# A fused cross-attention kernel: the loop's steps in a new order, the values of block 29 in other PSUM banks, and a new order on the way out

## The chip, the core and the metric

The kernel runs on one core of one Trainium2 chip. The metric is device time in microseconds (us) of one execution, the median of three. The core's engines are called PE (TensorE, matrix products), DVE (VectorE), ACT (ScalarE), POOL (GpSimd) and SP (SyncE, whose queue issues nearly all DMAs here). Each engine works off its own instructions in the order in which they were written; instructions of different engines are tied by semaphores alone.

## What is computed

Sixteen sequences of 1024 rows and 512 features (`x`) attend to a context of 64 rows each. Queries come from `x`, keys and values from the context, both after a layer norm whose scale and shift are made from a conditioning vector. There are 16 heads of 32 features. The result is projected and added to `x`. All is float32.

```python
xq  = ada_ln(x_q,  silu(t) @ Wss_q  + bss_q)
xkv = ada_ln(x_kv, silu(t) @ Wss_kv + bss_kv)
q   = (xq @ Wq + bq).reshape(B, Lq, 16, 32)
k,v = split(xkv @ Wkv + bkv)
scores = einsum('bqhd,bkhd->bhqk', q, k) / sqrt(32)
out = einsum('bhqk,bkhd->bqhd', softmax(scores), v).reshape(B, Lq, 512)
return x_q + (out @ Wp + bp)
```

## The kernel before, in words

The queries are cut into 32 blocks of 512 rows (two for each sequence), called by their numbers 0 to 31. A block goes through these stages:

- **load and norm**: `load_x` (1 MB by DMA), `q_stats` (DVE), `q_scale` (ACT, then four tiny POOL operations), `hidden` (ACT, four pieces).
- **turn**: `turn` (DVE, four pieces) transposes 32x32 squares into the tile `ht`, of which there is one. `move` (16 DMAs of 64 KB on SP's queue) carries `ht` into the tile `xt` of turned features, of which there are two. `scale_features` (ACT, four pieces) applies scale and shift to `xt`, and `feature_sums` (POOL, four pieces) forms the sums and differences for the next stage.
- **queries**: the 512x512x512 product is made of seven half-size products (Strassen-Winograd). `query_product(n, k)` for k = 1 to 7 is one of them on PE, called q1 to q7 here. They are summed in two PSUM banks: q1, q6, q5 and q3 in bank 0; q2, and after it q7 and q4, in bank 1. `query_seed` (ACT) copies bank 0 into bank 1 between q1 and q2. `query_out` (ACT) and `query_added` (DVE) take the results to the tiles `qt`. q7 begins a new sum in bank 1, so it has to wait for `query_out(n, 2)`, which reads q2's result there.
- **scores**: `score_products` (PE) for halves w = 0 and 1 into the PSUM pool `ps_s` (two tiles of two banks each). `copied` and `copied_bank` bring them to SBUF (ACT, one quarter on DVE), `maximum` and `maximum_copied` (DVE) take maxima, `exchanged` (ACT) and `maxima` (DVE, with a spread to full size) finish them, `subtract` (POOL) subtracts, `weights` (ACT) is the exponential, `row_total` (DVE) the sums, `sums_moved` (five DMAs), `inverse` and `spread_rows` (DVE) the reciprocals.
- **values**: `mix` (PE) multiplies weights and values. In the loop its four results go to the four product banks (`apart=False`), before the loop and after it to the two tiles of `ps_s`. `divided_bank` or `divided` (DVE) multiplies with the reciprocals into the tile `ot`.
- **projection**: again seven half-size products, `product(b, k)`, p1 to p7 here, with `row_sums` (POOL) for their operands, `biased` and `product_seed` (ACT) to fill banks ahead, and `take` (ACT) with `joined` (POOL), or `added` (DVE), to add results to the residual tile `r`. `joined` of 4 and `added` of 3 also issue the stores.

After a start of 142 us in which the stages fill, a loop of 28 steps works on five blocks at a time. In step `i` it has a = i-1 (second half of the scores, softmax), b = i-2 (values, projection), n = i+1 (queries), f = i+2 (features scaled and summed) and i+3 (norm, turn, move). The order of the calls is written out by hand and kept as written. What follows the loop, for blocks 29 to 31, is called the tail; there y = 30 and z = 31.

On PE a step is: scores of a (second half), mix of b, scores of i (first half), then seven q and seven p in some order, with q3 at the end. `move` of a step cannot begin before q3, which still reads the tile that it fills; SP's queue holds it back until then, and all that SP has behind it.

Of the kernel before, what the change touches and what calls it, by code (L numbers as in the profile page):

```python
# [20 lines left out]
def cross_attention_block(  # L21
# [729 lines left out]

    def weights(i, w):
        p = s_tiles[i, w]
        nc.scalar.activation(p, p, AF.Exp, scale=SCALE)  # L754
# [686 lines left out]
    for i in range(3, NB - 1):  # L1441
# [53 lines left out]
        if next_x:
            q_stats(i + 4, (3,))
        if more:
            turn(i + 3, (1,))
        maximum(i, 0, 1)
        weights(a, 1)  # L1500
        joined(b, 2, 0)
        row_total(a, 1)
        product(b, 6)
        product(b, 7)
        if i == NB - 3:
            load_residual(NB - 1)
        take(b, 6, 2)
# [5 lines left out]
        query_added(n, 5)
        sums_moved(a)
        if more:
            turn(i + 3, (3,))
        take(b, 7, 1)
        joined(b, 6, 2)
        exchanged(i, 0)
        if more:  # L1520
            turn(i + 3, (0,))
        if more:
            turn(i + 3, (2,))
        joined(b, 7, 1)
        take(b, 5, 3)
        if f < NB:
            scale_features(f, (2,))
        if f < NB:
            scale_features(f, (3,))
        joined(b, 5, 3)  # L1530
        if f < NB:
            feature_sums(f, nc.gpsimd, (0,))
        if next_x:
            q_stats(i + 4, (0,))
# [31 lines left out]
    maximum(y, 1, 0)
    copied(y, 1, 0)
    maximum(y, 1, 1)
    exchanged(y, 1)
    weights(y, 0)  # L1570
    biased(y - 1, 2)
    mix(y - 1)
    maxima(y, 1)
    divided(y - 1, (1,))
    divided(y - 1, (0,))
    row_total(y, 0)
# [145 lines left out]
```

## Time and profile before

| what | number |
|---|---|
| time, median of three runs | 1009.05 us (1008.04 to 1010.91) |
| time of the profiled execution | 1009.7 us |
| its span, first to last instruction | 1007.9 us |
| mean granted clock of PE | 0.995 |
| PEld busy (weight loads, beside PE) | 767.2 us (76%) |
| DVE busy | 927.2 us (92%) |
| ACT busy | 781.3 us (78%) |
| POOL busy | 852.8 us (85%) |
| start, to the first step of the loop | 0 to 142.35 us |
| loop, 28 steps | 142.35 to 944.53 us |
| tail | 944.53 us to the end |

Busy shares are means over stages. Whether an engine bounds a stage is read from stretches of the time line: from the length of one step, from what an engine waited for, and from what released it. The profile names instructions by line, output and input; buffer numbers are left out in it (`pq` is any bank of a query product, `pp` of a projection product, `ps` scores, `po` values, `mb` the spread maxima, `lt` the row sums).

### The profile page before, as it was taken

The numbers are of one execution on the slowest core, as the hardware profiler recorded it, in microseconds if no ns is written. First come the engines' busy times: TensorE is split into PE (matmuls) and PEld (weight loads), VectorE is DVE, ScalarE is ACT, GpSimd is POOL, SyncE is SP. The second block draws the span as 40 slices with busy tenths as digits, with TensorE's granted clock in tenths as the row PEclk, the third lists the DMA queues.
The fourth block names the chain that finished last, engine by engine and source line by source line (L and its number), as shares of the span: only waits on it lengthen the run. The fifth ranks groups of instructions, "written<-read, shape, count | busy, mean of one in ns | idle before, by whom it ended". The sixth has DMA issues, their size and how long they took to land.

```text
span 1007.9 us, 18000 instructions
## 1 busy us (share of the span) xinstructions
PE 987.9 (98%) x6088; PEld 767.2 (76%) x6088; DVE 927.2 (92%) x1221; ACT 781.3 (78%) x1459; POOL 852.8 (85%) x635
## 2 busy tenths in 40 slices
PE   8999999999999999999999999999999999999888
PEld 6878777787777777877777778777777788777567
DVE  6789999999999999999999999999999999887885
ACT  3689768788788888888888788888888888866550
POOL 2566688899999998999998899999999999988684
PEclk9999999999999999999999999999999999999899
DMA  9584553444544544545444545455444544443113
GB/s 322 181 228 132 160 182 108 155 155 147 161 139 143 153 159 158 165 137 167 149 144 133 161 160 164 135 166 154 148 132 161 160 158 128 131 128 129 47 48 131
DMA packets 111803, 151.71 MB, mean 151 GB/s; under 512 B 29624, under 2 KB 45008, under 8 KB 111712
## 3 DMA queue, kind: packets, MB, share of 16 engines
q1 hardware_dynamic: 111024, 149.75, 47.5%
q8 instruction: 48, 0.79, 0.3%
q0 software_dynamic: 256, 0.52, 0.2%
q14 instruction: 43, 0.35, 0.1%
q10 hardware_dynamic: 432, 0.30, 0.1%
HBM read 80.26 MB, written 35.65 MB: 115 GB/s over the span
## 4 chain that ended last, share of the span: by engine, by line
PE 63%; SPq 11%; DVE 8%; ACT 5%; POOL 5%; DMA 4%; issue 3%; DVEq 0%; POOLq 0%; ACTq 0%
PE pp L939 25%; PE pq L555 25%; SPq L402 10%; PE ps L675 4%; PE po L841 3%; DMA xt<-ht 2%; DVE lt L763 2%; POOL r L985 1%; ACT qt L596 1%; POOL xt L511 1%; POOL xt_sums L511 1%; PE pv_B L555 1%; PE pk_A L555 1%; ACT taken L980 1%; PE pk_B L555 1%
## 5 line engine op out<-in xcount | busy, mean ns | idle before, releaser
L750 POOL TENSOR_TENSOR s<-s,mb 128x2048 f32<-128x2048 f32 x64 | 290.8, 4543 | 26.2 <-DVE mb L733 23.8
L985 POOL TENSOR_TENSOR r<-r,taken 128x512 f32<-128x512 f32 x148 | 188.4, 1274 | 48.0 <-ACT taken L980 47.7
L939 PE MATMUL pp<-w_p_sb,ot 128*128 128x256 f32 x760 | 182.0, 384 | 0.0
L939 PEld LDWEIGHTS pp<-w_p_sb,ot 128*128 128x128 f32 x760 | 146.1, 193 | 22.9 <-issue 2.3
L763 DVE TRANSPOSE_TENSOR_REDUCE lt<-s 128x64 f32<-128x2048 f32 x64 | 146.3, 2286 | 8.8 <-ACT s L754 8.4
L733 DVE STREAM_TRANSPOSE mb<-m 128x2048 f32<-128x2048 f32 x64 | 147.9, 2311 | 6.7
L980 ACT COPY taken<-pp 128x512 f32<-128x512 f32 x148 | 86.7, 586 | 83.8 <-PE pp L939 83.0
L754 ACT ACTIVATE s<-s 128x2048 f32<-128x2048 f32 x64 | 122.2, 1910 | 11.7 <-POOL s L750 11.0
L555 PE MATMUL pq<-xt_sums,w_q_sums 128*128 128x256 f32 x512 | 122.3, 382 | 4.5 <-ACT qt L596 4.3
L555 PE MATMUL pq<-xt,w_q_sb 128*128 128x256 f32 x512 | 124.1, 385 | 0.0
L939 PE MATMUL pp<-WT,ot 128*128 128x256 f32 x512 | 121.2, 380 | 1.5 <-ACT pp L887 0.8
L555 PEld LDWEIGHTS pq<-xt,w_q_sb 128*128 128x128 f32 x512 | 94.7, 190 | 36.0 <-DVE ot L813 22.7
L939 PE MATMUL pp<-WT,s 128*128 128x256 f32 x512 | 121.0, 379 | 1.1 <-DVE r L964 1.1
L555 PE MATMUL pq<-xt,w_q_sums 128*128 128x256 f32 x512 | 121.0, 379 | 0.0
L596 ACT ACTIVATE qt<-pq,bias_t 128x256 f32<-128x256 f32 x256 | 106.5, 468 | 13.9 <-PE pq L555 13.9
L713 ACT COPY s<-ps 128x1024 f32<-128x1024 f32 x100 | 100.7, 1008 | 20.7 <-PE ps L675 17.4
L555 PEld LDWEIGHTS pq<-xt_sums,w_q_sums 128*128 128x128 f32 x512 | 96.0, 190 | 22.9 <-ACT qt L596 10.5
L460 ACT ACTIVATE xt<-xt,ss_q 128x512 f32<-128x512 f32 x124 | 97.8, 812 | 15.7 <-DMA xt<-ht 14.7
L939 PEld LDWEIGHTS pp<-WT,ot 128*128 128x128 f32 x512 | 97.0, 190 | 16.1 <-ACT pp L887 1.6
L939 PEld LDWEIGHTS pp<-WT,s 128*128 128x128 f32 x512 | 97.2, 190 | 15.2 <-issue 2.0
L555 PEld LDWEIGHTS pq<-xt,w_q_sums 128*128 128x128 f32 x512 | 97.3, 190 | 13.2
L351 ACT ACTIVATE x<-x,rstdq 128x512 f32<-128x512 f32 x128 | 97.6, 812 | 1.1 <-POOL rstdq L326 1.1
(175 smaller groups left out, 1694.6 us busy)
## 6 DMA issues: line engine op xcount, KB each, us to landing
x<-in_x_dram SPq DMA_DIRECT2D x32, 1024.0 KB, 5.2
r<-in_x_dram SPq DMA_DIRECT2D x32, 1024.0 KB, 5.1
out_dram<-r SPq DMA_DIRECT2D x62, 512.0 KB, 3.7
xt<-ht SPq DMA_DIRECT2D x488, 64.0 KB, 2.0
wss_kv<-in_L_xcond_Wss_kv_dram SPq DMA_DIRECT2D x4, 512.0 KB, 5.0
wss_q<-in_L_xcond_Wss_q_dram SPq DMA_DIRECT2D x4, 512.0 KB, 9.4
ltd<-lt SPq DMA_DIRECT2D x32, 64.0 KB, 1.5
vr<-ltd SPq DMA_DIRECT2D x126, 16.0 KB, 1.7
```

The costliest lines, as they stand in the source:

```text
L351: nc.scalar.activation(dst, src, AF.Identity, bias=rstd[:, 1, j : j + 1], scale=rstd[:, 0, j : j + 1])
L402: (nc.gpsimd if two and g % 2 else nc.sync).dma_start(xt[32 * k : 32 * k + 32, g], ht[32 * g : 32 * g + 32, k].rearrange("p c t b -> p c ( ...
L460: nc.scalar.activation(xt[:, :, c, :], xt[:, :, c, :], AF.Identity, scale=ss["q"][:, c, b : b + 1], bias=ss["q"][:, NC + c, b : b + 1],)
L555: nc.tensor.matmul(out_, lhsT=lhsT, rhs=rhs, start=new and m == 0 and c == 0, stop=c == HC - 1, skip_group_check=True,)
L596: nc.scalar.activation(dst, src, AF.Identity, bias=bq_t[:, o : o + 1])
L713: nc.scalar.copy(s_tiles[i, z][:, 2 * e : 2 * e + 2, :], s_banks[i, z][e])
L733: nc.vector.transpose(t, src.unsqueeze(2).to_broadcast([P, HPC * NJ, 32]))
L750: eng.tensor_tensor(s_tiles[i, w], s_tiles[i, w], mb_tiles[i, w], ALU.subtract)
L754: nc.scalar.activation(p, p, AF.Exp, scale=SCALE)
L763: nc.vector.tensor_reduce(lt_tiles[i][:, :, w, :], s_tiles[i, w].rearrange("p r (j a) -> p r j a", a=32), AX.X, ALU.add, apply_transpose=True,
L939: nc.tensor.matmul(acc[products_of(i, n)][:, t * HO : (t + 1) * HO], lhsT=rows[:, c, t * P : (t + 1) * P], rhs=cols[:, c, :], start=new an ...
L985: nc.gpsimd.tensor_add(r, r, taken[i][:, slot, :].rearrange("p (t h) -> p t h", t=2))
```

## The change

The change does not touch the start. It writes the calls of the loop and of the tail in another order, and changes three things beside it: block 29's values go to the product banks (`mix(y - 1, False)` with four calls of `divided_bank`), `divided_bank` gets the homes of the `ot` tiles that `divided` had, and there is a helper `subtracted` that nothing calls. The numbers and kinds of the loop's calls stay the same.

```diff
+    def subtracted(i, w, e):
+        rs = slice(2 * e, 2 * e + 2)
+        nc.vector.tensor_tensor(s_tiles[i, w][:, rs, :], s_banks[i, w][e], mb_tiles[i, w][:, rs, :], ALU.subtract)
...
     def divided_bank(i, w, d):
         if i not in ot_tiles:
-            ot_tiles[i] = opool.tile([P, NC, TB], F32, tag="ot", name=f"ot_{i}")
+            pool, tag = {NB - 3: (kvpool, "KA"), NB - 2: (big, "big2")}.get(i, (opool, "ot"))
+            ot_tiles[i] = pool.tile([P, NC, TB], F32, tag=tag, name=f"ot_{i}")
...
-        load_residual(a)
+        copied_bank(a, 1, 2, nc.scalar)
         copied(a, 1, 0)
         copied_bank(a, 1, 3, nc.vector)
-        copied_bank(a, 1, 2, nc.scalar)
         mix(b, False)
...
-    mix(y - 1)
+    mix(y - 1, False)
+    score_products(z, 0)
+    divided_bank(y - 1, 1, 1)
+    divided_bank(y - 1, 0, 0)
+    divided_bank(y - 1, 1, 0)
     maxima(y, 1)
-    divided(y - 1, (1,))
-    divided(y - 1, (0,))
```

**Place 1: PE in the step i = 22.** These are the first seven of the fourteen products of the step before the change; `pq_23_1` and `pq_23_2` are the banks of block 23's queries, `pp_20` those of block 20's projection, and the row with `pq_23_7` is q7.

```order
L555 MATMUL pq_23_1_6368<-xt_23_6028,w_q_sb_99 128x256 x4
L939 MATMUL pp_20_1_6376<-w_p_sb_102,ot_20_6352 128x256 x4
L555 MATMUL pq_23_1_6368<-xt_sums_544,w_q_sums_125 128x256 x4
L939 MATMUL pp_20_2_6399<-w_p_sb_102,ot_20_6352 128x256 x4
L555 MATMUL pq_23_2_6378<-xt_23_6028,w_q_sb_99 128x256 x4
L555 MATMUL pq_23_1_6368<-xt_23_6028,w_q_sums_125 128x256 x4
L555 MATMUL pq_23_7_6439<-xt_sums_544,w_q_sums_125 128x256 x4
```

The same seven places after the change (what was line 555 stays, the projection's line is now 944):

```order
L555 MATMUL pq_23_1_6364<-xt_23_6043,w_q_sb_99 128x256 x4
L944 MATMUL pp_20_1_6373<-w_p_sb_102,ot_20_6362 128x256 x4
L555 MATMUL pq_23_1_6364<-xt_sums_544,w_q_sums_125 128x256 x4
L555 MATMUL pq_23_2_6379<-xt_23_6043,w_q_sb_99 128x256 x4
L944 MATMUL pp_20_2_6396<-w_p_sb_102,ot_20_6362 128x256 x4
L944 MATMUL pp_20_1_6373<-WT_1309,s2_20_6430 128x256 x4
L555 MATMUL pq_23_7_6451<-xt_sums_544,w_q_sums_125 128x256 x4
```

q7 stays in seventh place; q2 moved from the fifth to the fourth, so that two products instead of one lie between q2 and q7, and q5 gave its place to p6. The other seven are p6, p7, p5, q4, p3, p4, q3 before, and p5, q5, p7, p3, q4, p4, q3 after.

**Place 2: ACT in the same step.** From `query_seed` to the exponential of the step's second half, before the change; L460 is `scale_features` of block 24, and the row of `qt_23_0` is `query_out(n, 2)`, for which q7 waits.

```order
L567 COPY pq_23_2_6378<-pq_23_1_6368 128x512
L742 COPY m2_21_1_6325<-m2_21_1_6325 32x64 x4
L893 COPY pp_20_2_6399<-pp_20_1_6376 128x512
L754 ACTIVATE s_21_0_6110<-s_21_0_6110 128x2048
L596 ACTIVATE qt_23_1_6412<-pq_23_1_6368,bias_t_119 128x2x4x32 x2
L980 COPY taken_20_6419<-pp_20_2_6399 128x512
L460 ACTIVATE xt_24_6283<-xt_24_6283,ss_q_473 128x4x128
L887 COPY pp_20_7_6431<-b_p_sb_101 128x512
L596 ACTIVATE qt_23_0_6411<-pq_23_2_6378,bias_t_119 128x2x4x32 x2
```

After the change the same stretch of ACT, on to the first `scale_features`:

```order
L596 ACTIVATE qt_23_1_6416<-pq_23_1_6364,bias_t_119 128x2x4x32 x2
L596 ACTIVATE qt_23_0_6415<-pq_23_2_6379,bias_t_119 128x2x4x32 x2
L985 COPY taken_20_6428<-pp_20_2_6396 128x512
L892 COPY pp_20_7_6432<-b_p_sb_101 128x512
L351 ACTIVATE x_25_6024<-x_25_6024,rstdq_6241 128x512
L985 COPY taken_20_6428<-pp_20_1_6373 128x512
L758 ACTIVATE s_21_1_6326<-s_21_1_6326 128x2048
L460 ACTIVATE xt_24_6298<-xt_24_6298,ss_q_473 128x4x128 x2
```

`scale_features` stood ahead of `query_out(n, 2)` and now stands six rows behind it. On SP the stores of `added(b, 3)` and `joined(b, 4)` and `load_x` now stand ahead of `move`, where before only `load_x` did.

**Place 3: DVE at the head of the tail.** Before the change, from the maxima of block 30 to the second row sums of block 30 (L824 is `divided`, both banks of a half at once):

```order
L691 TENSOR_REDUCE m2_30_1_8482<-ps_30_1_0_8472 128x32
L691 TENSOR_REDUCE m2_30_1_8482<-ps_30_1_1_8473 128x32
L724 TENSOR_REDUCE m_30_1_8513<-m2_30_1_8482 128x64
L733 STREAM_TRANSPOSE mb_30_1_8515<-m_30_1_8513 128x2048
L824 TENSOR_TENSOR ot_29_8517<-po_29_1_8496,vb_29_8468 128x1024
L824 TENSOR_TENSOR ot_29_8517<-po_29_0_8495,vb_29_8468 128x1024
L763 TENSOR_REDUCE lt_30_8520<-s_30_0_8327 128x4x16
L691 TENSOR_REDUCE m2_31_0_8533<-ps_31_0_0_8523 128x32
L691 TENSOR_REDUCE m2_31_0_8533<-ps_31_0_1_8524 128x32
L763 TENSOR_REDUCE lt_30_8520<-s_30_1_8483 128x4x16
```

After the change (L818 is `divided_bank`, one bank at a time):

```order
L691 TENSOR_REDUCE m2_30_1_8484<-ps_30_1_0_8474 128x32
L691 TENSOR_REDUCE m2_30_1_8484<-ps_30_1_1_8475 128x32
L818 TENSOR_TENSOR ot_29_8526<-po_29_1_1_8497,vb_29_8468 128x512
L818 TENSOR_TENSOR ot_29_8526<-po_29_0_0_8494,vb_29_8468 128x512
L818 TENSOR_TENSOR ot_29_8526<-po_29_1_0_8496,vb_29_8468 128x512
L724 TENSOR_REDUCE m_30_1_8530<-m2_30_1_8484 128x64
L733 STREAM_TRANSPOSE mb_30_1_8532<-m_30_1_8530 128x2048
L691 TENSOR_REDUCE m2_31_0_8524<-ps_31_0_1_8515 128x32
L691 TENSOR_REDUCE m2_31_0_8524<-ps_31_0_0_8514 128x32
L818 TENSOR_TENSOR ot_29_8526<-po_29_0_1_8495,vb_29_8468 128x512
L767 TENSOR_REDUCE lt_30_8552<-s_30_0_8323 128x4x16
```

The divisions moved ahead of the spread maxima of block 30, but the one of `po_29_0_1` moved behind the maxima of block 31; p1 of block 29 reads it in its second matmul. On PE the order of the tail's head is the same in both: scores of 30, mix of 29, scores of 31, p1.

More of the change, by code (lines that the diff above doesn't have):

```diff
@@ L1497, in cross_attention_block @@
         if more:
[L1498 to L1507, printed above, removed]
+            turn(i + 3, (0,))
+        take(b, 5, 3)
         query_out(n, 7)
+        query_added(n, 5)
+        take(b, 7, 1)
+        product(b, 3)
         row_sums(b, 1, (1,))
-        product(b, 5)
+        joined(b, 6, 2)
+        joined(b, 7, 1)
+        if more:
+            turn(i + 3, (3,))
+        maxima(i, 0)
+        if next_x:
+            q_scale(i + 4)
+        sums_moved(a)
+        if f < NB:
+            scale_features(f, (1,))
+        query_product(n, 4)
+        product(b, 4)
         if f < NB:
             scale_features(f, (0,))
[L1513 to L1521, printed above, removed]
+        joined(b, 5, 3)
+        copied(i, 0, 1)
+        copied(i, 0, 0)
+        if f < NB:
+            feature_sums(f, nc.gpsimd, (0,))
+        query_added(n, 4)
         if more:
             turn(i + 3, (2,))
[L1524 to L1534, printed above, removed]
+        added(b, 3)
         if f < NB:
@@ L1582, in cross_attention_block @@
+    maxima(y, 1)
+    biased(y - 1, 2)
     copied(z, 0, 1)
     maximum(z, 0, 1)
-    weights(y, 1)
-    take(y - 1, 1, 0)
-    row_total(y, 1)
-    exchanged(z, 0)
-    row_sums(y - 1, 0, (1,))
-    copied(z, 0, 0)
-    row_sums(y - 1, 1, (0,))
-    maxima(z, 0)
-    joined(y - 1, 1, 0)
+    maximum(z, 0, 0)
+    subtract(y, 1)
+    divided_bank(y - 1, 0, 1)
+    row_sums(y - 1, 0, (0,))
+    row_sums(y - 1, 0, (1,))
+    weights(y, 0)
+    exchanged(z, 0)
+    weights(y, 1)
+    row_sums(y - 1, 1, (0,))
@@ L1602, in cross_attention_block @@
-    biased(y, 2)
     maximum(z, 1, 0)
-    biased(y - 1, 3)
-    product(y - 1, 7)
-    copied(z, 1, 0)
-    maximum(z, 1, 1)
-    exchanged(z, 1)
-    inverse(y)
-    row_sums(y - 1, 1, (1,))
-    product(y - 1, 5)
-    take(y - 1, 5, 1)
+    exchanged(z, 1)
+    maxima(z, 1)
+    inverse(y)
+    joined(y - 1, 2, 1)
+    row_sums(y - 1, 1, (1,))
+    copied(z, 1, 0)
+    copied(z, 1, 1)
+    subtract(z, 1)
+    take(y - 1, 5, 1)
+    mix(y)
+    spread_rows(y, (0,))
+    weights(z, 0)
+    take(y - 1, 7, 2)
@@ L1613, in cross_attention_block @@
+    spread_rows(y, (1,))
+    divided(y, (0,))
+    divided(y, (1,))
     product(y - 1, 3)
[L1614 to L1617 removed]
     product(y - 1, 4)
[L1619 to L1633 removed]
@@ L1634, in cross_attention_block @@
[L1634 to L1655 removed]
+    row_total(z, 0)
+    weights(z, 1)
+    row_total(z, 1)
@@ new lines, in cross_attention_block @@
+    product(y, 1)
+    product(y, 2)
+    added(y, 1)
+    added(y, 2)
+    row_sums(y, 0, (0,))
+    biased(y, 3)
+    row_sums(y, 0, (1,))
+    mix(z)
+    joined(y - 1, 7, 2)
+    row_sums(y, 1, (0,))
+    row_sums(y, 1, (1,))
+    product(y, 6)
+    sums_moved(z)
+    product(y, 7)
+    added(y, 6)
+    added(y, 7)
+    joined(y - 1, 5, 1)
+    take(y - 1, 3, 2)
+    inverse(z)
+    product(y, 5)
+    biased(z, 2)
+    spread_rows(z, (0,))
+    take(y, 5, 1)
+    take(y - 1, 4, 0)
+    joined(y - 1, 6, 3)
@@ L1669, in cross_attention_block @@
-    product(z, 6)
     biased(z, 3)
-    row_sums(z, 1, (1,))
-    added(y, 3)
     product(z, 7)
@@ L1675, in cross_attention_block @@
     added(z, 7)
+    added(y, 3)
     product(z, 5)
+    product(z, 4)
     added(z, 5)
-    product(z, 4)
     product(z, 3)
```

170 lines of the change are left out of this document (74 added, 96 removed).

## The prediction

> All times are of the profiled execution: 1009.7 us, span 1007.9. It stood 0.65 us above the median of three (1009.05).
>
> **What bounds the kernel now.** I read the page's engine shares, then the stretches of the time line, then PE's own rows, then the waits, then the chain.
>
> ```profile
> PE 987.9 (98%) x6088; PEld 767.2 (76%) x6088; DVE 927.2 (92%) x1221; ACT 781.3 (78%) x1459; POOL 852.8 (85%) x635
> ```
> PE is busy 98% of the span, so there is little to gain: 20 us of idle in all. The stretches (length, then busy time of PE, PEld, DVE, ACT and POOL, then PE's granted clock) say where.
>
> ```profile
> 142.35:170.69 28.34, 28.34 (x177) 22.15 (x177) 27.44 (x38) 22.96 (x42) 23.75 (x20) 1.00 0.43 137
> 170.69:200.23 29.54, 28.60 (x177) 22.07 (x176) 28.03 (x36) 23.78 (x44) 26.13 (x20) 1.00 0.46 148
> 142.35:915.81 773.46, 768.98 (x4754) 596.76 (x4753) 737.90 (x928) 637.67 (x1172) 701.75 (x506) 1.00 0.48 149
> 915.81:944.53 28.72, 28.72 (x178) 22.33 (x177) 23.86 (x24) 17.57 (x31) 22.82 (x14) 1.00 0.23 78
> 944.53:982.47 37.94, 31.32 (x217) 17.81 (x217) 32.73 (x27) 22.56 (x34) 31.97 (x16) 0.87 0.18 59
> 945.68:982.33 36.65, 30.20 (x200) 17.55 (x200) 32.09 (x25) 21.73 (x32) 30.68 (x15) 0.86 0.18 61
> 982.47:1003.73 21.26, 21.25 (x96) 17.96 (x96) 12.90 (x17) 2.28 (x4) 11.27 (x10) 1.00 0.37 132
> ```
> The first two are the loop's first and second step, from one score product of PE to the next. The first takes 28.34 us with PE never idle: that is what PE's work of a step needs, the floor. The third row holds 27 steps: 773.46 - 27 x 28.34 = 8.28 us above the floor. The fourth is the last step: 28.72, 0.38 above. So the loop has **8.66 us** to give, no more.
>
> ```profile
> 142.35 1.11 PE L675 MATMUL ps<-qt,K_A 32*64 32x512 f32 x16
> 146.32 1.99 PE L555 MATMUL pq<-xt,w_q_sb 128*128 128x256 f32 x8
> 858.35 1.11 PE L675 MATMUL ps<-qt,K_B 32*64 32x512 f32 x16
> 886.68 1.11 PE L675 MATMUL ps<-qt,K_B 32*64 32x512 f32 x16
> 186.22 1.99 PE L555 MATMUL pq<-xt_sums,w_q_sums 128*128 128x256 f32 x8 [0.94 <-ACT qt L596]
> PE pq L555 <- ACT qt L596: 4.3, 9, 0.9
> ```
> The first two rows are the start of the loop and the first of its products, 3.97 later. From 858.35 to 886.68 is the last of eleven steps (of 27) at the floor, the first being that from 142.35. The row at 186.22 is q7, the seventh product of the second step. It waited 0.94 us for `query_out(n, 2)`. The last row, from the list of waits, is the only wait of PE in the loop: 9 times 4.3 us together; the rest of the 8.28 us is the refill after it and waits too short to be listed. The chain shows what holds it, in the step from 743.59:
>
> ```profile
> 743.96 0.28 SPq L402
> ...
> 754.10 2.06 DMA xt<-ht
> ...
> 756.38 0.81 ACT xt L460
> 757.20 0.48 ACT pp L887
> 757.68 0.77 ACT qt L596 x2
> ...
> 758.49 1.56 PE pq L555 x6
> ```
> `move` begins when q3 of the step before is done, issues sixteen DMAs in 10.1 us, and the last lands 2.06 us later. `scale_features` waits for it on ACT, and the `query_out` that q7 needs stands behind it in ACT's queue.
>
> **The change in the loop.** Set a step's start at 0. PE's fourteen products fill the time from 3.97 to 28.34, 1.74 each (1.73 from start to start), and q7 is seventh in both orders, at 14.5. Before, `query_out(n, 2)` stood behind a landing at 12.2 to 13.4; now it stands behind the first exponential, q2 and nothing of the move. On ACT: the seed copy after q1 (6.0 to 6.6), `exchanged` to 7.65, two pieces to 8.95, `weights(a, 0)` to 10.9, two `query_out` to 12.5: 2 us before q7. `scale_features` now follows `weights(a, 1)`, at 17.3 at the earliest. So this stall goes: **-8.28, and -0.38** for the last step, whose move is long over. What is late next decides whether the floor is reached, and here three queues are nearly full.
>
> ```profile
> L750 POOL TENSOR_TENSOR s<-s,mb 128x2048 f32<-128x2048 f32 x64 | 290.8, 4543 | 26.2 <-DVE mb L733 23.8
> L763 DVE TRANSPOSE_TENSOR_REDUCE lt<-s 128x64 f32<-128x2048 f32 x64 | 146.3, 2286 | 8.8 <-ACT s L754 8.4
> L733 DVE STREAM_TRANSPOSE mb<-m 128x2048 f32<-128x2048 f32 x64 | 147.9, 2311 | 6.7
> L754 ACT ACTIVATE s<-s 128x2048 f32<-128x2048 f32 x64 | 122.2, 1910 | 11.7 <-POOL s L750 11.0
> 658.46 10.75 SPq L402 DMA_DIRECT2D xt<-ht  x16
> 543.82 11.33 SPq L402 DMA_DIRECT2D xt<-ht  x16
> x<-in_x_dram SPq DMA_DIRECT2D x32, 1024.0 KB, 5.2
> ```
> DVE is busy 27.44 us of a floor step, and with the gaps between its instructions some 27.95 (start to start in the step from 658.30, its waits taken out). 0.4 us may be waited. I laid its 36 calls in the new order end to end. `copied_bank` starts at 1.8, for it now waits for ACT's copy of the neighbouring quarter; the spread maxima end 8.8 later, at 10.6; POOL subtracts for 4.54 to 15.3, ACT takes 1.91 to 17.25, and DVE stands before `row_total(a, 1)` at 17.2: 0.1 waited. `query_added(n, 4)` would come at 24.8 and has to wait for q4, now twelfth instead of eleventh, until 25.0: 0.2 waited. Five us of work follow, to 30.0, which is 1.7 of the next step, and `copied_bank` there can start at 1.8: 0.1 waited. The sum fits, by less than 0.1 us. It has a cushion: PE needs that copy only for the scores at 2.92, and it ends at 2.5.
>
> POOL: `joined(b, 7)` waits for p7 and starts at 22.15. Then four small norm operations, `joined` 5, two sums, `joined` 4, one sum, a subtract, one sum and two `row_sums` take 16.85 and end at 39.0, 10.66 of the next step; the spread maxima that it needs then come at 10.6 to 10.8. That too just fits. `joined(b, 4)` ends at 1.1 instead of 0.5.
>
> SP: `move` stands behind the store of that `joined`, so it starts at 1.65 instead of 0.15. With issues of 10.0 to 11.33 and 2.0 to land it is done at 13.7 to 15.0. `scale_features` (17.3) has 2.3 us to spare; `turn(1)` on DVE, which refills `ht`, comes at 15.5 and has 0.5. `load_x`, 5.2 to land, is issued at 27.6 instead of 22.9 and its first reader comes at 7 of the next step: 2.3 spare.
>
> The unknown here is what such tight queues cost. Bounds: nothing, and all of the 8.66 (the wait goes elsewhere). I take nothing, because eleven of 27 steps before reached the floor with DVE as full as now. `subtracted`, and the homes of `ot`, cost nothing: no instruction.
>
> **The tail.** Before, PE waits twice at its head and works slowly around these waits, then waits for DVE:
>
> ```profile
> 948.03 3.43 PE L841 MATMUL po<-s,V_B 64*32 64x512 f32 x32 [2.39 <-ACT s L713]
> 953.06 2.87 PE L675 MATMUL ps<-qt,K_B 32*64 32x512 f32 x16 [1.60 <-DVE ot L824]
> 955.86 6.40 PE L939 MATMUL pp<-w_p_sb,ot 128*128 128x256 f32 x16
> 982.47 1.96 PE L939 MATMUL pp<-WT,s 128*128 128x256 f32 x8 [1.11 <-DVE r L964]
> 945.68 2.44 DVE L691 TRANSPOSE_TENSOR_REDUCE m<-ps 128x32 f32<-128x1024 f32 x2 [0.62 <-PE ps L675]
> 951.82 2.32 DVE L824 TENSOR_TENSOR ot<-po,vb 128x1024 f32<-128x1024 f32 x2
> 971.16 2.33 DVE L805 STREAM_TRANSPOSE vb<-iv 128x1024 f32<-128x1024 f32 x2
> 948.16 1.00 ACT L742 COPY m<-m 32x64 f32<-32x64 f32 x4 [0.18 <-DVE m L691]
> ```
> In the new order `mix` of 29 needs no score buffer and follows at once (no wait of 2.39, no slow 3.43), scores of 31 follow at 3.4 instead of 8.5. But the gain isn't kept: p1's second matmul needs the division of `po_29_0_1`, and on DVE six things now stand ahead of it: two maxima, three divisions, the spread maxima, two more maxima. From 1.1: 2.4 + 1.8 + 2.6 + 2.3 + 0.6 gives 10.8. p1 goes on at 10.9; before, it began at 11.3. So PE's early start is worth 0.4 us.
>
> What ends the stretch is DVE. From 945.68 to 982.33, where p6 of block 30 is released, it was busy 32.09 of 36.65 us. Its work stays (four divisions of a bank, 2.4, for two of two banks, 2.32); what changes is its waits. Laid end to end: 10.8, row sums 13.0, spread maxima of 31 15.6, row sums 17.8, maxima 20.1, a wait of 1.0 for `exchanged` (ACT, 1.00), spread maxima 23.8, reciprocals with two spreads and two divisions 29.4, two row sums 33.8, one `added` 34.4. p6 starts at 34.5 instead of 37.94: **-3.5 us**. Its other inputs are there: scores of 31 by 18, where DVE asks at 17.8; the exponentials at 14.5, 25.4 and 31.2; p2's end at 17; `mix` of 31 ends at 33.6; `row_sums` at 34.2. Then twelve products, 21.26 before, 20.7 plus 0.35 for the last division now. Bounds: -5.1 (DVE without any wait, 4.56, and 0.5 of the products), and +1 (slow products hold `take` and the scores of 31).
>
> The long hold has a price that I weigh by rows: between 4.6 and 10.9 PE has 0.4 us of work.
>
> ```profile
> 946.00:948.00 2.00, 0.00 (x0) 0.00 (x0) 2.00 (x2) 1.85 (x2) 2.00 (x1) 0.92 1.01 383
> 956.00:958.00 2.00, 2.00 (x5) 1.64 (x6) 2.00 (x3) 2.00 (x2) 1.92 (x3) 0.50 0.00 0
> ```
> After 2.4 us of waiting the clock fell from 0.92 to 0.50, and p1 and p2 took 6.40 us at it instead of 3.45. I count p1 and p2 as slow again; their end at 17 then costs 0.3 at most, since scores of 31 wait for a copy until 15.4 and DVE until 17.8. The Trainium skill ("TensorE: Matmul & The Clock Gate", section "HAM oscillation — how this bites in real kernels") speaks against this order: a gap of more than about 3.4 us puts the clock to half. The trace agrees on the half (0.50), and it shows it already after 2.39 us.
>
> **Sum.** 1009.7 - 8.28 - 0.38 - 3.5 = 997.5 us. Against the median it would be 996.9; I leave the 0.65 in, for waits of under 0.1 us in queues as full as these.
>
> **The rivals.**
> - *A full queue sets a new step* (0.17). DVE or POOL misses its fit by 0.1 to 0.3 us, and each step is that much longer. For it: margins of under 0.1. Against: the 0.4 us before PE asks for the copy. At 0.2 it costs 27 x 0.2 = 5.4: 1002.9 us.
> - *The clock stays low in the tail* (0.08). By the slow row a product takes 3.2 instead of 1.73; if it stays so for p6, p7 and p5 as well, these end 4.4 us later, `mix` of 30 and the divisions with them, and the tail gains nothing: 1001.0 us. The skill's page, in the section "What's actually happening", gives about 3.4 us of work until the clock returns; the slow row of 6.40 speaks for longer, though not for as long as this needs.
> - *The change doesn't do what it says* (0.05). The move is late, `scale_features` is late with it, and POOL's sums hold q6 or q7 as ACT did: loop as before, tail -3.5: 1006.2 us. Against: 2.3 us to spare.
> - *Slower* (0.07). `turn(1)` stands before half of DVE's step and waits for the last of sixteen DMAs, which now start 1.5 us later, behind a store of 512 KB and a load of 1 MB. If landing passes 15.85, the step grows by the rest; from 16.3 the kernel is slower than before. At 16.7 it is 28 x 0.85 = 23.8 longer than the floor: 997.5 + 23.8 = 1021.3 us. The longest issue before (11.33) gives 15.0.
>
> **How the numbers follow.** Forecast 997.5, with 0.60 for 994.5 to 1001. Better than 994.5 would need the tail's whole -5.1 and more: 0.03. With the clock case and two thirds of the first rival, up to 1004.5, the range 994.5 to 1004.5 holds 0.79. About 0.3%, 3 us, is what a measurement of this kernel can tell from no change. Faster than 1006.0: 0.60 + 0.17 + 0.08 + 0.03 = 0.88; within: 0.05; slower: 0.07.
>
> **What would show it.** Right: steps of 28.34 between score products, no wait of PE's `pq` on ACT's `qt`; `scale_features` without a wait for the DMA; p6 of block 30 some 34.5 us after the last step; one wait of about 5 us at p1 of block 29. Wrong: a wait of DVE's `ht` on the move, a wait of PE's `ps` on DVE's copy, or steps that are all longer by the same amount.

## The result, and the profile after

The changed kernel takes **1000.2 us** (median of 4 runs, 999.02 to 1001.5) where the kernel before took 1008.67 (1008.04 to 1010.91): a ratio of 0.9912, with a 95% interval of 0.9891 to 0.9934. That is 8.5 us faster, where 12.2 had been forecast (1009.7 to 997.5, of the profiled execution); 1000.2 lies inside the range. The profiled execution took 1001.5 us, its span is 998.8.

From the page of the kernel after, the engines' busy time:

```profile
PE 984.1 (99%) x6088; PEld 771.0 (77%) x6088; DVE 920.1 (92%) x1223; ACT 784.5 (79%) x1459; POOL 847.2 (85%) x635
```

Then the stretches of the time line (length, busy time of PE, PEld, DVE, ACT and POOL, then PE's granted clock): the loop's 28 steps, the last step's start to p6 of block 30, and from there to the end of PE's work.

```profile
143.56:939.22 795.66, 794.07 (x4929) 620.42 (x4928) 755.88 (x951) 658.22 (x1203) 719.42 (x519) 1.00 0.49 148
939.22:974.02 34.80, 28.26 (x217) 17.56 (x217) 32.92 (x29) 21.56 (x32) 31.25 (x16) 0.90 0.16 54
974.02:995.05 21.03, 21.03 (x96) 17.96 (x96) 12.97 (x17) 3.43 (x6) 12.00 (x10) 1.00 0.36 132
```

The loop's floor is 28 x 28.34 = 793.52. Before, the loop took 802.18, 8.66 above it; now it is 795.66, **2.14 above it**. The tail to p6 of block 30 fell from 37.94 to 34.80. The start, whose code is the same, took 143.56 instead of 142.35. So the span's 9.1 us are +1.21 (start), -6.52 (loop) and -3.79 (all of the tail, 63.37 to 59.58). Among the thirteen other profiles of this study, the loop begins anywhere from 141.71 to 143.87 behind the same start: that part of the difference belongs to the execution, not to the change.

The waits of the kernel after (engine, output and line, what it waited for: us in total, times, longest):

```profile
DVE ht L382 <- DMA xt<-ht: 10.6, 14, 1.2
DVE s L701 <- ACT s L701: 3.0, 12, 0.8
PE ps L675 <- DVE s L701: 1.4, 4, 0.5
```

The wait of `pq` for `query_out` (4.3 us in 9 places before) is gone from this list. In its place stand the two signs that were to show the forecast wrong: `turn(1)` on DVE waits for the move, and PE's scores wait for DVE's copy of a quarter. One step of the time line shows how they hang together (start, length, queue or engine, what):

```profile
313.25 0.41 SPq L108 DMA_DIRECT2D x<-in_x_dram  x1
314.88 0.38 SPq L992 DMA_DIRECT2D out_dram<-r  x1
315.31 13.42 SPq L402 DMA_DIRECT2D xt<-ht  x16
330.36 0.71 DVE L382 STREAM_TRANSPOSE ht<-x 128x512 f32<-128x512 f32 x1 [1.02 <-DMA xt<-ht]
344.51 0.65 DVE L701 COPY s<-ps 128x512 f32<-128x512 f32 x1
345.21 1.12 PE L675 MATMUL ps<-qt,K_A 32*64 32x512 f32 x16 [0.26 <-DVE s L701]
```

`load_x` goes out 2.06 us ahead of the move, `joined`'s store 0.43 ahead. The move's sixteen issues then take 13.42 us; in the kernel before they took 10.0 to 11.3. `turn(1)` waits 1.02 for the last landing, DVE is late through the rest of the step, its copy ends late in the next, and PE waits there. The table of DMAs (KB each, median us from issue to landing) shows the load itself stretched, from 5.2 to 7.3; the move's single DMAs went from 2.0 to 2.4.

```profile
x<-in_x_dram SPq DMA_DIRECT2D x32, 1024.0 KB, 7.3
xt<-ht SPq DMA_DIRECT2D x488, 64.0 KB, 2.4
```

In the tail, PE and DVE of the kernel after:

```profile
942.73 1.24 PE L675 MATMUL ps<-qt,K_B 32*64 32x512 f32 x16 [0.51 <-ACT s L713]
950.09 6.04 PE L944 MATMUL pp<-w_p_sb,ot 128*128 128x256 f32 x14 [4.64 <-DVE ot L818]
957.31 2.38 DVE L691 TRANSPOSE_TENSOR_REDUCE m<-ps 128x32 f32<-128x1024 f32 x2 [0.28 <-PE ps L675]
960.78 0.29 DVE L724 TENSOR_REDUCE m<-m 128x64 f32<-128x128 f32 x1 [1.09 <-ACT m L742]
974.02 1.97 PE L944 MATMUL pp<-WT,s 128*128 128x256 f32 x8 [0.60 <-DVE r L969]
```

There is one long hold, of 4.64 us, at p1 of block 29, which goes on 10.87 after the last step; the products behind it are slow (6.04 us for fourteen matmuls, where the eight at 974.02 take 1.97). DVE itself waits only 0.28 and 1.09.

### The profile page after: what moved, and what is told of

Its sections match the earlier page's. It is cut to its first block, busy times and chain, and to the rows that moved or that the text cites. A ratio compares the mean times of both kernels' runs of the same rounds, so it can differ in the third digit from the quotient of the medians.

```text
span 998.8 us, 17928 instructions
## 1 busy us (share of the span) xinstructions
PE 984.1 (99%) x6088; PEld 771.0 (77%) x6088; DVE 920.1 (92%) x1223; ACT 784.5 (79%) x1459; POOL 847.2 (85%) x635
## 4 chain that ended last, share of the span: by engine, by line
PE 81%; DMA 6%; DVE 6%; SPq 3%; POOL 2%; issue 2%; ACT 0%; DVEq 0%; POOLq 0%; ACTq 0%
PE pq L555 33%; PE pp L944 31%; PE ps L675 5%; PE po L846 4%; DMA out_dram<-r 3%; SPq L402 2%; DVE lt L767 2%; PE pv_B L555 1%; PE pk_A L555 1%; PE pk_B L555 1%; PE pv_A L555 1%; POOL r L990 1%; DVE vb L803 1%; DMA vr<-ltd 1%; DMA xt<-ht 1%
## 5 line engine op out<-in xcount | busy, mean ns | idle before, releaser
L596 ACT ACTIVATE qt<-pq,bias_t 128x256 f32<-128x256 f32 x256 | 103.8, 468 | 40.2 <-PE pq L555 38.4
L944 PE MATMUL pp<-WT,ot 128*128 128x256 f32 x512 | 116.5, 379 | 0.0
L351 ACT ACTIVATE x<-x,rstdq 128x512 f32<-128x512 f32 x128 | 100.5, 815 | 1.8 <-POOL rstdq L326 1.1
L713 ACT COPY s<-ps 128x1024 f32<-128x1024 f32 x100 | 97.7, 1006 | 2.9 <-DVE m L691 2.1
L382 DVE STREAM_TRANSPOSE ht<-x 128x512 f32<-128x512 f32 x124 | 85.4, 693 | 15.1 <-DMA xt<-ht 10.6
```

The costliest lines, as they stand in the source:

```text
L351: nc.scalar.activation(dst, src, AF.Identity, bias=rstd[:, 1, j : j + 1], scale=rstd[:, 0, j : j + 1])
L382: nc.vector.transpose(ht_tiles[i][:, :, :, t, :].rearrange("p k c b -> p c k b"), x_tiles[i][:, t, :].rearrange("p (c k b) -> p c k b", c= ...
L596: nc.scalar.activation(dst, src, AF.Identity, bias=bq_t[:, o : o + 1])
L713: nc.scalar.copy(s_tiles[i, z][:, 2 * e : 2 * e + 2, :], s_banks[i, z][e])
L944: nc.tensor.matmul(acc[products_of(i, n)][:, t * HO : (t + 1) * HO], lhsT=rows[:, c, t * P : (t + 1) * P], rhs=cols[:, c, :], start=new an ...
```

## The experiments

The theory after this reading: the loop's gain comes from one call, `scale_features(f, (1,))`, which no longer stands ahead of `query_out(n, 2)` on ACT; what the loop keeps above its floor is the move's late landing; and the tail's gain is DVE's order. The rivals: the new order is needed as a whole; the rest of the loop's loss has another cause; the tail gains by the banks. Kernels with the same number in the third column ran on one chip, beside the same executions of before. The column "loop" is the loop's length less 793.52, and "p6" the time from the last step's start to p6 of block 30, both of the profiled execution.

| kernel | us, median | before, on that chip | ratio (95%) | loop | p6 |
|---|---|---|---|---|---|
| before, profiled | | | | 8.66 | 37.94 |
| after | 1000.20 | 1008.67 | 0.9912 (0.9891 to 0.9934) | 2.14 | 34.80 |
| before_scale_behind | 1001.52 | 1011.09 | 0.9907 (0.9885 to 0.9928) | 1.00 | 36.94 |
| before_new_tail | 1008.58 | 1011.09 | 0.9976 (0.9964 to 0.9989) | 11.33 | 34.39 |
| after_turn_behind | 998.58 | 1011.09 | 0.9887 (0.9858 to 0.9915) | 2.14 | 34.39 |
| after_store_behind | 999.28 | 1011.09 | 0.9884 (0.9862 to 0.9906) | 2.41 | 34.38 |
| after_again | 999.44 | 1010.07 | 0.9897 (0.9880 to 0.9914) | 1.82 | 34.66 |
| before_scale_new_tail | 998.88 | 1010.07 | 0.9892 (0.9873 to 0.9912) | 1.16 | 34.39 |
| after_load_early | 997.98 | 1010.07 | 0.9879 (0.9861 to 0.9898) | 0.06 | 34.39 |
| after_divided_near | 1001.86 | 1010.07 | 0.9923 (0.9906 to 0.9939) | 0.76 | 36.73 |
| after_scale_ahead | 1099.06 | 1010.80 | 1.0873 (1.0850 to 1.0897) | 100.40 | 34.81 |
| after_old_tail_banks | 1000.06 | 1010.80 | 0.9897 (0.9881 to 0.9914) | 0.46 | 36.38 |
| after_load_earliest | 1164.60 | 1008.37 | 1.1547 (1.1522 to 1.1571) | 168.48 | 34.38 |
| after_load_early_2 | 996.65 | 1008.37 | 0.9888 (0.9871 to 0.9906) | 0.06 | 34.39 |

Before itself stood between 1008.37 and 1011.09 from chip to chip, so kernels are compared by ratio, or within one chip.

### One call moved in the kernel before

```diff
-        if f < NB:
-            scale_features(f, (1,))
         row_sums(b, 0, (0,))
         row_sums(b, 1, (0,))
         query_product(n, 2)
         subtract(a, 1)
         biased(b, 3)
         query_out(n, 2)
+        if f < NB:
+            scale_features(f, (1,))
```

> The kernel before with one call moved: `scale_features(f, (1,))` goes from ahead of `query_out(n, 2)` on ACT to right behind it; the tail is the old one. Theory (the loop's gain is this one call's place): the wait of q7 for ACT goes, the 27 steps lose most of their 8.28 us, 1000.5 to 1002 us. Rival (the new order is needed as a whole, since the late pieces now hold POOL's sums and with them q6 or q7): less than 2 us gained, 1006.5 to 1008.7.

Measured 1001.52 us, 0.9907 of before: by the ratio as large a gain as that of the whole change, though on this chip the old loop may have had more to give (it stood 11.33 above its floor in the next experiment, where the first profile has 8.66). The trace is the better witness. The stretches of this kernel (the loop, then the old tail to p6 of block 30):

```profile
143.02:937.54 794.52, 794.48 (x4929) 620.42 (x4929) 759.30 (x951) 656.93 (x1203) 724.67 (x519) 1.00 0.48 148
937.54:974.48 36.94, 29.91 (x218) 17.10 (x217) 32.54 (x27) 22.55 (x34) 31.95 (x16) 0.86 0.19 61
```

26 of its 27 steps behind the first take 28.33 or 28.34. The only other one, the last, takes 29.44, since DVE's `inverse` waits ahead of it for the row sums' DMA, and DVE's copy of a quarter behind it is late. The kernel before has the same wait at the same place, ahead of its last step (the second row is of that kernel):

```profile
907.68 0.29 DVE L790 TENSOR_REDUCE iv<-vr 128x64 f32<-128x128 f32 x1 [2.17 <-DMA vr<-ltd]
914.67 0.29 DVE L790 TENSOR_REDUCE iv<-vr 128x64 f32<-128x128 f32 x1 [1.46 <-DMA vr<-ltd]
```

So the 8.28 us of the first 27 steps are this call's place, and these steps reach the floor without the rest of the new order. The last step's 0.38 is another wait. It is there in the four kernels with the old loop order (28.72, 29.44, 29.44 and 29.59 us) and gone in all ten with the new one (28.34).

### The same call put back in the kernel after

```diff
+        if f < NB:
+            scale_features(f, (1,))
         query_out(n, 2)
...
         sums_moved(a)
-        if f < NB:
-            scale_features(f, (1,))
```

> After, with the one piece `scale_features(f, (1,))` put back ahead of `query_out(n, 2)`; all else stays in the new order. Theory (this call's place is the whole of the loop's stall, and the later move makes the old place worse than it was): the move lands at some 16.6 of the step, the piece and `query_out` take 1.2 more, q7 begins at 17.5 to 18 instead of 14.5 in each of the 25 steps that have a move: 2.5 to 3.5 us each, 1062 to 1088 us. Rival (the new order has made room on ACT elsewhere, q7 waits as seldom as before): 1007 to 1010 us.

Measured 1099.06 us. The list of waits and the loop's stretch:

```profile
PE pq L555 <- ACT qt L596: 65.4, 25, 3.9
```

```profile
142.19:1036.11 893.92, 824.35 (x4929) 629.94 (x4929) 759.29 (x951) 654.96 (x1203) 719.76 (x519) 0.98 0.45 132
```

q7 waits in each of the 25 steps, 2.6 us in the mean, as the theory had it. The price of it was set too low: the loop is 100.4 above its floor, not 62 to 88. PE is also busy 30.3 us longer with the same matmuls (824.35 against 794.07), at a mean granted clock of 0.98 instead of 1.00. Here the waits cost half as much again as their length.

### The tail of after behind the loop of before

The edit is the tail's part of the change, with nothing of the loop's.

> The loop of before with the whole tail of after. Theory (the tail's gain is its own, the loop's is another): p6 of block 30 starts 34.5 to 35 after the last step, 1004.5 to 1005.2 us, 3.5 to 4.1 less than before. Rival (the new tail lives on what the new loop leaves it, the residual loaded ahead or the last step's shorter queues): half of it or less, 1006.7 to 1008.7.

```profile
141.71:946.56 804.85, 798.64 (x4929) 619.10 (x4928) 762.43 (x951) 655.05 (x1203) 724.58 (x519) 1.00 0.48 146
946.56:980.95 34.39, 27.55 (x217) 16.60 (x216) 32.21 (x29) 21.46 (x32) 30.86 (x15) 0.90 0.20 66
```

The tail alone gives 2.5 us (1011.09 to 1008.58; by the interval 1.1 to 3.6), between the two expectations. In the trace p6 of block 30 starts at 34.39, 3.55 sooner than in the first profile of before and 2.55 sooner than in `before_scale_behind`, which has the same old tail; the old loop happened to stall more in this execution (11.33 above its floor, 8.66 in the one before), which says how far such a stall varies by itself.

### Two ways to take the wait of `turn` away

`after_turn_behind` asks later:

```diff
-        if more:
-            turn(i + 3, (1,))
...
         maximum(i, 0, 0)
+        if more:
+            turn(i + 3, (1,))
```

> After, with `turn(i + 3, (1,))` moved on DVE behind the next maximum (`maximum(i, 0, 0)`), so that it asks for the moved tile some 1.2 us later. Theory (the 2.1 us above the floor that the loop kept are the move's late landing: DVE waits, then its copy of a quarter, then PE's scores): the waits of `ht` for the move fall from 10.6 us to under 3, PE's wait for DVE's copy goes, 1.5 to 2.1 us less than after: 998.1 to 998.7. Rival (DVE is simply full, or POOL's subtraction sets the pace): the waits change their name, 999.7 to 1000.7.

`after_store_behind` lets the move go first (`stored` issues what `joined` issued itself):

```diff
-        joined(b, 4, 0)
+        joined(b, 4, 0, False)
...
             move(i + 3)
+        stored(b, 4)
```

> After, with the store of `joined(b, 4)` issued behind the move instead of ahead of it; POOL's order stays. Theory: the move begins at 0.15 of the step instead of 1.67, the waits of `ht` go, 1.5 to 2.1 us less than after: 998.1 to 998.7. What slows the sixteen issues (11.4 to 13.4 us where they took 10.0 to 11.3): if the store ahead does it, they are back at 10.0 to 11.3; if the load of x that is still under way does it, they stay at 11.4 or more and only the earlier start helps. Rival (not the landing): 999.7 to 1000.7.

They are 0.9887 and 0.9884 of before, where after was 0.9912 and, on another chip, 0.9897: the intervals overlap, so the times tell no gain. The traces do tell something. In both, DVE's waits for the move are gone, and the loop is no shorter (2.14 and 2.41 above the floor; after has 2.14 and, in a later profile, 1.82). So the wait of `turn` wasn't the cause but one of two victims. The other, in `after_turn_behind`, and in the fourth row in `after_store_behind`:

```profile
198.52 0.94 SPq L108 DMA_DIRECT2D x<-in_x_dram  x1
200.73 13.65 SPq L402 DMA_DIRECT2D xt<-ht  x16
207.63 0.69 DVE L308 BATCH_NORM_STATS2 bs<-x 128x6 f32<-128x512 f32 x1 [1.37 <-DMA x<-in_x_dram]
208.59 0.69 DVE L308 BATCH_NORM_STATS2 bs<-x 128x6 f32<-128x512 f32 x1 [2.23 <-DMA x<-in_x_dram]
```

The load of x, issued at 198.52, has landed only at 207.6, and `q_stats` waits 1.37 us for it. The issues in `after_store_behind`:

```profile
313.26 0.47 SPq L108 DMA_DIRECT2D x<-in_x_dram  x1
314.24 12.52 SPq L402 DMA_DIRECT2D xt<-ht  x16
326.86 0.52 SPq L996 DMA_DIRECT2D out_dram<-r  x1
```

```profile
x<-in_x_dram SPq DMA_DIRECT2D x32, 1024.0 KB, 7.5
```

No store stands between the load and the move here, and the issues still take 12.52; the load takes 7.5. So `joined`'s store isn't what slows them. That the load under way is, the traces show by two moves that have none beside them: the last two of the loop. In after, with the same stores ahead:

```profile
882.94 0.39 SPq L992 DMA_DIRECT2D out_dram<-r  x1
883.43 10.80 SPq L402 DMA_DIRECT2D xt<-ht  x16
```

These two take 11.09 and 10.80 us in after (11.09 and 11.18 in `after_store_behind`), where the 24 moves with a load beside them take 12.7 in the mean, 11.4 to 13.7 (12.6, 11.5 to 14.8, in `after_store_behind`). The load's own stretch has less proof: the move lies beside it, but so does the store of `added`, issued some 0.5 us ahead of it.

### The load earlier

```diff
+        if more:
+            turn(i + 3, (2,))
+        if i < NB - 5:
+            load_x(i + 5)
         query_added(n, 4)
-        if more:
-            turn(i + 3, (2,))
         added(b, 3)
...
-        if i < NB - 5:
-            load_x(i + 5)
```

> The changed kernel itself, as the yardstick for the three beside it (another chip's DMAs may land otherwise). Two theories of what the change is worth: if before's stall is longer on a chip where before is slower (1011.1 us where it was 1008.7), after stands at 999.5 to 1001 us whatever before takes; if all scales, it stays at 0.991 of before.

> After, with `turn(i + 3, (2,))` ahead of `query_added(n, 4)` on DVE and `load_x(i + 5)` right behind that turn, ahead of the store of `added(b, 3)` on SP; the order of move and `joined`'s store stays. Theory (what the loop keeps above the floor comes from the load of x that overlaps the move and makes both late): the load is issued at some 25.2 of the step instead of 27.5 and lands before the move begins; the move's sixteen issues take 10.0 to 11.3 us again instead of 11.4 to 13.4, DVE waits neither for the move (10.6 us in after) nor for x, the loop is under 0.7 us above 28 x 28.34: 1.3 to 2 us less than after. Rival (the landing is late because the store stands ahead, or because the issues are slow whatever lies beside them): within 0.5 us of after, with the same waits.

The edit also brings the load ahead of the store of `added`. After stood at 999.44 us, 0.9897 of before, which doesn't tell its two theories apart. With the load early it is 997.98 (996.70 to 998.34, where after has 998.31 to 1001.05). The views of the kernel with the load early: the loop and the tail, one step's issues, the load's time to land, and DVE's wait.

```profile
143.55:937.13 793.58, 793.58 (x4929) 620.39 (x4928) 756.21 (x951) 659.25 (x1203) 719.32 (x519) 1.00 0.49 149
937.13:971.52 34.39, 27.68 (x218) 16.93 (x217) 32.81 (x29) 21.47 (x32) 30.86 (x15) 0.90 0.17 55
```

```profile
310.89 0.39 SPq L108 DMA_DIRECT2D x<-in_x_dram  x1
315.25 11.55 SPq L402 DMA_DIRECT2D xt<-ht  x16
```

```profile
x<-in_x_dram SPq DMA_DIRECT2D x32, 1024.0 KB, 6.1
```

```profile
DVE ht L382 <- DMA xt<-ht: 0.9, 1, 0.9
```

The load now leads the move by 4.36 us instead of 2.06. The issues of the 24 moves with a load last 11.0 us in the mean (10.2 to 11.7), where they lasted 12.7 in after: no longer than moves without a load. The waits for the move fall from 10.6 us to 0.9, and PE is busy in every instant of the loop: 793.58 of 793.58. A second execution on another chip, beside the next experiment, gave the same:

> The kernel with the load at 25.7 of the step once more, beside the one with the load at 23, on the same chip. If its loop stands at the floor by its order and not by the luck of one execution, it is again 0.3 us or less above 28 x 28.34, and the time 0.986 to 0.9895 of before.

```profile
141.90:935.48 793.58, 793.58 (x4929) 620.38 (x4928) 756.26 (x951) 659.34 (x1203) 719.54 (x519) 1.00 0.50 148
```

996.65 us, 0.9888 of before. By the ratios this isn't told from after; by the loop it is, which stood at 0.06 twice, and at 0.46 to 2.14 in the four kernels that share after's loop unchanged. It has the lowest median of the study.

The four profiles with after's loop (two of after, and one each of two kernels of which more below) differ in the tail alone, and so show the same loop four times. The longer DVE waited for the move, the longer the loop:

| kernel | DVE's waits for the move | loop above the floor |
|---|---|---|
| after | 10.6 us in 14 places | 2.14 |
| after_again | 10.7 in 14 | 1.82 |
| after_divided_near | 6.5 in 12 | 0.76 |
| after_old_tail_banks | 4.5 in 9 | 0.46 |
| after_load_early, twice | 0.9 and 0.6, in 1 | 0.06 |

### The load earlier still

```diff
         if more:
             turn(i + 3, (3,))
+        if more:
+            turn(i + 3, (2,))
+        if i < NB - 5:
+            load_x(i + 5)
         maxima(i, 0)
         if next_x:
             q_scale(i + 4)
         sums_moved(a)
```

> After, with `turn(i + 3, (2,))` and `load_x(i + 5)` right behind `turn(i + 3, (3,))`, ahead of `maxima(i, 0)`: the load goes out at some 23 of the step, as in before, while the move still stands behind `joined`'s store. Theory (the overlap of the load with the move sets how long the move's issues take): the load lands in 5.2 to 5.5 us again, the sixteen issues take 10.0 to 11.3 us, mean 10.6 or less, where they took 11.0 with the load at 25.7 and 12.2 to 12.5 with the load at 27.5; DVE waits for no move, and the loop is at its floor as in the kernel with the load at 25.7: within 0.5 us of that kernel. Rival (the store ahead of the move slows the issues, or their length varies of itself): issues of 11.5 us or more in the mean.

1164.6 us: a miss, by a queue that the expectation had left out. The waits:

```profile
SPq L108 <- DVE ht L382: 356.4, 27, 16.6
DVE iv L794 <- DMA vr<-ltd: 132.2, 24, 6.7
PE ps L675 <- DVE s L701: 86.7, 24, 4.8
```

`load_x` now stands ahead of `sums_moved` on SP. It has to wait there for the turn that frees its tile, up to 16.6 us, and the row sums' five DMAs wait behind it; `inverse` on DVE waits up to 6.7 for them, then the copy of the quarter is late, and PE waits 3.6 us in each of 24 steps. These 86.7 us are half of what the loop loses (962.0 us, 168.5 above its floor); PE is also busy 81 us longer than in after with the same matmuls, at a mean granted clock of 0.94. The move's issues take 11.1 in the mean, between the theory's 10.6 and the rival's 11.5, with the load landed 3 to 4.5 us before each move where the trace has both times: as long as the moves without a load in after. What parts them from the 10.6 of before, the two stores issued just ahead or the other traffic of these longer steps, is not shown.

### The loop of before, one call moved, and the tail of after

Two edits shown already: `scale_features(f, (1,))` behind `query_out(n, 2)`, and the tail's part of the change.

> The loop of before with `scale_features(f, (1,))` behind `query_out(n, 2)`, and the tail of after. Theory (the loop's gain is the place of this one call, the rest of the new order in the loop only costs): 26 of 27 steps at 28.34 and a tail of 59.5, together 1.1 us less in the loop than after: 0.5 to 1.5 us below after. Rival (the loop's new order is also worth something beside): 1 us or more above after.

998.88 us beside 999.44 of after on the same chip: 0.56 less, with ranges that overlap. The rival, 1 us or more above after, isn't seen. So the other moves within the loop's step are worth nothing that the times can show. In the traces they take the wait out of the last step (29.59 here, 28.34 in after) and cost about as much by the move's late landing in the others (1.16 above the floor here, 0.46 to 2.14 in the new order).

### The tail: where PE is held, and the banks

`after_divided_near` puts the fourth division next to the other three:

```diff
     divided_bank(y - 1, 0, 0)
+    divided_bank(y - 1, 0, 1)
     divided_bank(y - 1, 1, 0)
...
     subtract(y, 1)
-    divided_bank(y - 1, 0, 1)
```

> After, with `divided_bank(y - 1, 0, 1)` in the tail next to the three others, ahead of the spread maxima and two maxima of block 31. Theory (DVE's chain sets the tail; where PE waits in it is of no account): PE's wait of 4.64 us before p1 of block 29 shrinks by some 4, its clock stays high, p6 of block 30 starts within 0.6 us of where it did (34.8 after the last step): 0 to 0.6 us less than after. Rival (the hold and the slow clock behind it cost): 2 us or more less than after.

It is slower: 1001.86 (1000.57 to 1003.6) beside 999.44 (998.31 to 1001.05), and p6 of block 30 starts at 36.73 instead of 34.66. Both expectations are wrong. PE, ACT and DVE of this kernel, in order of time (the first row is the last part of the scores of 31):

```profile
954.27 1.99 PE L675 MATMUL ps<-qt,K_B 32*64 32x512 f32 x8 [5.27 <-ACT s L713]
959.98 0.59 ACT L985 COPY taken<-pp 128x512 f32<-128x512 f32 x1 [3.65 <-PE pp L944]
960.59 1.00 ACT L742 COPY m<-m 32x64 f32<-32x64 f32 x4
961.63 0.29 DVE L724 TENSOR_REDUCE m<-m 128x64 f32<-128x128 f32 x1 [2.93 <-ACT m L742]
```

The hold didn't shrink, it moved: p1 and p2 run at once, and the second half of the scores of 31 now waits 5.27 us for ACT's copy. The slow clock then falls on the product that `take` waits for on ACT (3.65), `exchanged` stands behind that `take`, and DVE waits 2.93 for it instead of 1.09. In after, the slow products are over before DVE asks for anything behind them.

`after_old_tail_banks` has after's loop and the old tail, with the banks alone changed:

```diff
     weights(y, 0)
-    biased(y - 1, 2)
-    mix(y - 1)
+    mix(y - 1, False)
     maxima(y, 1)
-    divided(y - 1, (1,))
-    divided(y - 1, (0,))
+    divided_bank(y - 1, 1, 0)
+    divided_bank(y - 1, 1, 1)
+    divided_bank(y - 1, 0, 0)
+    divided_bank(y - 1, 0, 1)
+    biased(y - 1, 2)
```

> After's loop with the tail of before, in which only the homes of block 29's values are changed: `mix(y - 1, False)`, four calls of `divided_bank` where the two of `divided` stood, and `biased(y - 1, 2)` behind them, since it fills a bank that they read. Theory (DVE's order sets the tail, the banks alone only let PE start sooner): PE's wait of 2.39 before the values of 29 goes, but p6 of block 30 stays at 37 to 38.5 after the last step: 2.5 to 3.5 us more than after, 1002 to 1003.5 us. Rival (the banks are what the tail gains by): p6 at 34.5 to 35.5, within 0.7 us of after.

```profile
143.78:937.76 793.98, 793.90 (x4930) 620.51 (x4929) 757.22 (x951) 659.04 (x1203) 719.63 (x519) 1.00 0.50 148
937.76:974.14 36.38, 28.12 (x218) 17.38 (x217) 33.27 (x29) 22.58 (x34) 32.04 (x16) 0.91 0.16 52
```

p6 starts at 36.38: between the theory (37 to 38.5) and the rival (34.5 to 35.5). The old tail gave 37.94 in before and 36.94 in `before_scale_behind`, so the banks give 0.6 to 1.6 us and the order of the calls another 1.6 to 2.0 (36.38 to 34.39 or 34.80). This split is rough: it rests on one profile of this kernel, and the old tail stood behind another loop. The time, 0.9897 of before as after had on another chip, doesn't show the difference; in this execution the loop was 0.46 above its floor, which makes up for it. The new order with block 29's values in their old homes was not tried.

## Why the prediction was right, and where it was not

- **The wait that goes.** "So this stall goes: -8.28, and -0.38 for the last step." The -8.28 is right, and shown twice: one call moved in before takes it away, and the same call put back in after brings it back, larger. The -0.38 came true by luck: it was no part of this stall but `inverse`'s wait for the row sums, which the call's place alone leaves (29.44 us in the last step) and which the forecast didn't look at.
- **What the tight queues cost.** "Bounds: nothing, and all of the 8.66 ... I take nothing." This is the term that was mis-sized: it measured 2.14 us in the profiled execution, and 0.46 to 1.82 in three others of the same loop. The reason given for nothing, that DVE was as full in steps at the floor, holds: with the load early DVE is just as busy (756.21 us in the loop against 755.88) and the loop stands at the floor. What failed lies on SP. "With issues of 10.0 to 11.33 ... it is done at 13.7 to 15.0", and "`load_x`, 5.2 to land ... 2.3 spare": both durations were read from a kernel in which the load lands as the move begins (0.83 us before it to 0.17 after, where the trace has both times), and the change itself puts the two side by side: the load now lands 4.1 to 5.8 us into the move. They became 11.4 to 13.7 and 7.3.
- **The slower rival** named the right mechanism, `turn(1)` waiting for the landing, but priced it as the same in all steps. DVE waited 14 times, 10.6 us together; PE had to wait for DVE's copy in 4 places, 1.4 us, since the copy had the 0.4 us to spare that the prediction counted.
- **The tail.** "p6 starts at 34.5 instead of 37.94: -3.5": it started at 34.80, p1 went on at 10.87 (10.9), and the slow products cost DVE 0.28 (0.3). The sum was right, its reading only in part. "What ends the stretch is DVE" holds for three of the ten profiles of this tail, after among them: in the seven others, with p6 at 34.38 or 34.39, it is released by POOL's `row_sums`, which the forecast had at 34.2. "So PE's early start is worth 0.4 us" is right for this order (p1 goes on at 10.87 instead of 11.33), but it isn't what the banks can give: in the old order, with the banks alone, p1 starts at 9.90, and p6 0.6 to 1.6 sooner. And where the hold falls is not free: next to another product it costs 2.1. The clock was read too simply as well: in before it was back at 0.99 from 952.53 to 954.53, and the slow products from 955.86 on followed a second fall, not the one that the hold of 2.39 brought.
- **The start** was taken as fixed; it was 1.21 us longer in this execution, and within 141.71 to 143.87 elsewhere.

Added up for the profiled execution: 997.5 forecast, plus 2.14 (loop), plus 1.21 (start), less 0.29 (of -3.79 instead of -3.5 in the tail), plus 0.9 (what lies outside the span, 2.7 instead of 1.8) gives 1001.5, the time it took.

## What to carry to other kernels

When a transfer is moved, its duration in the old profile holds only if the same things lie beside it in the new place: list what will be under way on the DMA engines at that time, as one lists what stands ahead in a queue. A wait on a landing belongs behind whatever the bounding engine needs next on the same queue; here the place of one call gave all that the times can show of the loop's gain. And a call that issues DMAs is moved past the issuing queue's other members too: here a load that had to wait up to 16.6 us for its tile held all that stood behind it.

## What the runs showed of the hardware

- A load of 1 MB and sixteen DMAs of 64 KB, issued 2 us apart from one queue, are both slower than apart: the load takes 7.3 instead of 5.2 us to land, the sixteen issues 12.7 instead of 10.6 us in the mean (over the 24 moves of either kernel with a load). With 4.36 us between them it is 6.1 and 11.0; the two moves of after without a load take 11.09 and 10.80. Of the move's DMAs in the loop, the slowest took 3.9 us to land in the kernel before, and in the kernel after (min, median and max):

```profile
DMA to landing us min/median/max: 1.9/2.3/8.1
```

  The Trainium skill ("Trainium Kernel Development and Optimization", section "Key Constraints") says that DMAs of all queues run on the same 16 DMA engines and interleave. The trace agrees, with 7.3 for 5.2. That the issuing of the later DMAs grows longer too is not in that sentence; the issue rows show it.
- In the tail PE's granted clock falls to 0.50 in the hold of 4.64 us and stays there through the first five microseconds of the work behind it, which begins at 950.09:

```profile
949.22:951.22 2.00, 1.13 (x3) 0.96 (x4) 2.00 (x3) 0.97 (x4) 2.00 (x1) 0.50 0.00 0
951.22:953.22 2.00, 2.00 (x6) 1.57 (x5) 1.90 (x3) 1.34 (x1) 1.92 (x3) 0.50 0.00 0
953.22:955.22 2.00, 2.00 (x6) 1.63 (x5) 2.00 (x2) 2.00 (x4) 2.00 (x2) 0.50 0.00 0
```

  The Trainium skill ("TensorE: Matmul & The Clock Gate", section "What's actually happening") has the window that decides run freely, so that the turning points vary from run to run. The trace agrees: in ten profiles with the same tail and the same hold (4.64 or 4.65 us) the fourteen products behind it took anything from 4.91 to 6.04 us. Up to 5.60 it cost nothing (p6 at 34.38 or 34.39); at 5.89, 6.04 and 6.04 p6 stood at 34.66, 34.80 and 34.81.
- A wait of 2.6 us need not lower the clock. In `after_scale_ahead` q7 of one step waits 2.64 us with dense work on both sides of it, and the granted clock stays at 1.00 (the first stretch lies within the wait):

```profile
314.00:316.00 2.00, 0.00 (x0) 0.00 (x0) 1.77 (x4) 1.34 (x3) 0.32 (x1) 1.00 0.65 153
316.00:318.00 2.00, 1.75 (x8) 1.44 (x8) 0.59 (x1) 1.97 (x5) 1.25 (x2) 1.00 0.97 371
```

  The mean over its loop is 0.98, so in other steps it does fall.
